# When an attention loop lets in its other work: pieces kept out of the steps in which VectorE masks both pairs

## The chip, the cores and the metric

The kernel runs on one core of one Trainium2 chip. The metric is the device time of one execution in microseconds (us): before the change the median of three runs is 4116.18 us (4115.72 to 4121.67). TensorE (PE) multiplies, VectorE (DVE), ScalarE (ACT) and GpSimd (POOL) work on what comes out, and SyncE (SP) issues transfers. GpSimd has no part in reading the accumulators: in this kernel it only works on tiles that ScalarE or VectorE has written.

## The reference

Three graph-attention layers and one closing layer work on 16 graphs of 1024 nodes with 128 features; one adjacency matrix serves all.

```python
# layers 0, 1, 2: eight heads of 16 features
Q = (h @ Wq).reshape(B, N, 8, 16); K = ...; V = ...
scores = jnp.einsum('bnhd,bmhd->bhnm', Q, K) / jnp.sqrt(16.)
attn = jax.nn.softmax(jnp.where(mask, -jnp.inf, scores), axis=-1)
x = _layer_norm(h + (einsum('bhnm,bmhd->bnhd', attn, V) @ Wo + bo), ln1_g, ln1_b)
x = _layer_norm(x + (jax.nn.relu(x @ W1 + b1) @ W2 + b2), ln2_g, ln2_b)
# layer 3: one head; the score is s_i + s_j through a leaky ReLU
h = x @ W;  e = leaky((h @ a_src)[:, :, None] + (h @ a_dst)[:, None, :])
out = layernorm(softmax(masked e) @ h + x)
```

## The kernel before

**Blocks and steps.** A block is one graph in one of the layers 0 to 2; there are 48, in groups of four graphs (`LANES`): layer 0 of four graphs, then layer 1 of the same four, then layer 2, then the next four graphs. A block has 32 steps: two groups of four heads (`g`) by two halves of the queries (`qh`) by eight tiles of 128 keys (`kt`), so that the step's number modulo 8 is its `kt`. The loop in lines 755 to 795 walks through all 1536 steps. In each it calls, in this order, `score_step`, `av_due` and `piece`.

**A step.** `score_step` (L411) makes two pairs of heads, each a 128x1024 tile of scores in one of three accumulator slots (`s`). A pair is masked in one of two ways. On GpSimd: ScalarE takes the exponential from the slot (L426), and GpSimd multiplies it with a 0/1 mask (L427). On VectorE: VectorE adds a large negative mask while it reads the slot (L429), and ScalarE takes the exponential later (L441). The second pair is always masked on VectorE. The first goes to GpSimd, but for three of the eight key tiles:

```python
BOTH_ON_DVE = (2, 5, 7)
on_pool = pp == 0 and kt not in BOTH_ON_DVE
```

So VectorE has two masks in steps with `kt` 2, 5 and 7 and one in the other five. `av_due` multiplies with the values, four steps later (`AHEAD`), into one accumulator (`acc`, a single buffer). After the last `kt` of a half, `finish` (L449) has VectorE transpose the sums out of it.

**The other work** is cut into pieces. A block's projections (`proj_tasks`, L353) are eight pieces for the next block: two transposes (`t0`), two halves each of K and Q (`split`, where ScalarE writes a rounded part `hi` and VectorE the rest `lo`), two halves of V. What follows a block's attention (`post_tasks`, L465) is eleven: `both` (transposes of the sums on VectorE), two halves of the output projection (`out_proj`: VectorE adds and takes statistics, GpSimd normalises), two transposes (`x1t`), four halves of the first feed-forward product (`ffn1`) and two of the second (`ffn2`). The closing layer (`last_tasks`, L537) is twelve for each graph. All pieces use the one accumulator bank `t` (L134): a piece on TensorE can't start before the last one has been read out of it.

**When a piece runs.** `put` appends pieces to a chain, with a gap in steps that each keeps to the one before. `piece` (L682) is called at the end of each step and takes the first piece, over the chains in order, whose gap has passed; at most one is taken. `need` (L687) takes pieces at once until a mark is reached. `proj_tasks` of the next block enter at the head in step 6. Line 780 asks for them to be done in step 19 (24 in the first block), and `stack` (L397) is emitted there: 16 transfers within the chip which lay `hi` and `lo` out for the first four heads of the next block.

The orders on TensorE and ScalarE are those of the program (`manual_schedule`). Those on VectorE, GpSimd and SyncE are made by a scheduler, with a head start for what frees the bank `t` (`soon`).

In most blocks that lie away from the closing layers, the rule gives this pattern ("." is no piece; `op` is `out_proj`, `f1` is `ffn1`; kt 2, 5 and 7 in brackets):

```
kt           0      1      (2)    3      4      (5)    6      (7)
step  0-7    .      .      .      .      .      both   op0    t0(0)
step  8-15   t0(1)  Wk0    op1    Wk1    .      Wq0    .      Wq1
step 16-23   x1t0   V0     V1     x1t1   f1     f1     f1     f1
step 24-31   ffn2   ffn2   .      .      .      .      .      .
```

Of the kernel before, what the change touches and what calls it, by code (L numbers as in the profile page):

```python
# [28 lines left out]
SOON = 120  # L29
LANES = 4  # L30
FIRST = 1
AHEAD = 4
BOTH_ON_DVE = (2, 5, 7)
TILES = {"w": 10, "x": LANES + 1, "last": 2}
# [77 lines left out]
def fast_path(ctx: ExitStack, tc: tile.TileContext, a: dict, out: bass.AP, flag):  # L112
# [3 lines left out]
    NT = N // P  # L116
# [40 lines left out]
    def fetch(b):  # L157
        def run():
            state["x", b] = load_x(b)
        return run  # L160
# [60 lines left out]
    def first_weights():  # L221
        W[0].update(load_layer(nc, nc.sync, const, a, 0, ("Wo", "b2", "W1", "b1", "W2", "ln1_g", "ln2_g")))
        norm_weights(nc.sync, 0)
# [5 lines left out]
    def other_weights():  # L229
        for l in range(1, L):  # L230
            W.append(load_layer(nc, nc.sync, const, a, l, [n for n in LAYER if n not in ("ln1_b", "ln2_b")]))
            norm_weights(nc.sync, l)
        nc.sync.dma_start(ln2_b_last, rows_of(a[f"L{L - 1}_gnn_ln2_b"]))
        for n in LAST:
            src = a[f"L3_gnn_{n}"]
            if n == "W":
                t = w_nodes[:, :D]
                nc.sync.dma_start(t, src)
            elif n in ("a_src", "a_dst"):
                t = const.tile([P, 1], F32, name=n)  # L240
                nc.sync.dma_start(t, src.rearrange("(p o) -> p o", o=1))
            else:
                t = const.tile([P, D], F32, name=n)
                nc.sync.dma_start(t, rows_of(src))
            wl[n] = t

    def biases():
        for l in range(L):
            if l:
                add_bias(nc.sync, "ln2_b", l - 1, "bo", l)  # L250
            add_bias(nc.sync, "ln1_b", l, "b2", l)

    def last_weights():
        a2 = const.tile([P, 2], F32)
        nc.vector.tensor_copy(a2[:, 0:1], wl["a_src"])
        nc.vector.tensor_copy(a2[:, 1:2], wl["a_dst"])
        ps = bank()
        nc.tensor.transpose(ps[:, :P], w_nodes[:, :D], identf)
        w3t = work.tile([P, P], F32, tag="row", name="w3t", bufs=2)
        nc.vector.tensor_copy(w3t, ps[:, :P])  # L260
        ps = bank()
        nc.tensor.matmul(ps[:, :2], w3t, a2, start=True, stop=True)
        nc.vector.tensor_copy(w_nodes[:, D:], ps[:, :2])
# [133 lines left out]
    def stack(m, g):  # L397

        for pp in range(2):
            for n, order in (("Wk", (0, 1, 0, 1)), ("Wq", (0, 0, 1, 1))):  # L400
                t = work.tile([P, N], F32R, tag=n, name=n, bufs=4)
                r0 = (g * J + 2 * pp) * HD
                for i, part in enumerate(order):
                    behind["stack"] = nc.sync.dma_start(t[i:P:4, :].bitcast(F32), state[n, m][part][r0:r0 + 2 * HD, :].bitcast(F32)).ins
                state[n, g, pp] = t
# [5 lines left out]
    def score_step(step):  # L411
        m, g, qh, kt = step
        e = e_tile()
        q0 = qh * 512
        for pp in range(2):
            q, k = state["Wq", g, pp], state["Wk", g, pp]
            ps = slot()
            for r in range(2):
                nc.tensor.matmul(ps[:, r * 512:(r + 1) * 512], k[64 * r:64 * r + 64, kt * P:(kt + 1) * P],  # L419
                                 q[64 * r:64 * r + 64, q0:q0 + 512], start=True, stop=True)  # L420
            ev = e[:, 2 * pp:2 * pp + 2, :]
            psv = ps.rearrange("p (r q) -> p r q", q=512)
            on_pool = pp == 0 and kt not in BOTH_ON_DVE
            m = (mask01 if on_pool else mask_add)[:, kt, q0:q0 + 512][:, None, :].to_broadcast([P, 2, 512])
            if on_pool:
                nc.scalar.activation(ev, psv, AF.Exp, scale=HD ** -0.5)  # L426
                behind["pool"] = nc.gpsimd.tensor_mul(ev, ev, m).ins  # L427
            else:
                behind["dve"] = nc.vector.tensor_add(ev, psv, m).ins  # L429
                masked.append((2 * step_no[0] + pp + (kt not in BOTH_ON_DVE), ev))  # L430
        step_no[0] += 1
        exponentials()
        return e
# [217 lines left out]
    blocks = [(b, l) for p in range(0, B, LANES) for l in range(L) for b in range(p, p + LANES)]  # L651
    chains = []
    done = {("fetch", b) for b in range(2)}
    now = [0]
# [3 lines left out]
    def put(tasks, mark, chain=None, first=False):  # L658

        if chain is None:  # L660
            chain = {"due": now[0], "queue": deque()}
            chains.insert(0 if first else len(chains), chain)
        for n, task in enumerate(tasks):
            chain["queue"].append(task + (mark if n == len(tasks) - 1 else None,))
        return chain

    def take(chain):

        gap, f, tiles, mark = chain["queue"][0]
        if any(free[t[1:]] == 0 for t in tiles.split() if t[0] == "+"):  # L670
            return False
        chain["queue"].popleft()
        f()
        for t in tiles.split():
            free[t[1:]] += -1 if t[0] == "+" else 1
        done.add(mark)
        chain["due"] = now[0]
        if not chain["queue"]:
            chains.remove(chain)
        return True  # L680

    def piece():  # L682
        for chain in chains:
            if now[0] >= chain["due"] + chain["queue"][0][0] and take(chain):
                return

    def need(mark):  # L687
        while mark not in done:
            first = next(c for c in chains if any(q[3] == mark for q in c["queue"]))
            assert take(first) or any(take(c) for c in list(chains) if c is not first)  # L690
# [63 lines left out]
    with tc.manual_schedule(engines={mybir.EngineType.PE, mybir.EngineType.Activation}):  # L754
        for m, (b, l) in enumerate(blocks):
            order = [(g, qh) for g in range(G) for qh in range(2)]
            if m in (0, len(blocks) - 1):
                order.sort(key=lambda x: x[1])
            for at, (g, qh, kt) in enumerate((g, qh, kt) for g, qh in order for kt in range(NT)):
                now[0] = n  # L760
                if at == (6 if m == 0 else 1):
                    stack(m, 1)
                if n == 6:
                    with tc.issue_after(behind["stack"]):
                        first_weights()
                        other_weights()
                if n == 20:
                    with tc.issue_after(behind["pool"]):
                        biases()
                if n == 40:  # L770
                    with tc.issue_after(behind["dve"]):
                        last_weights()
                if at == 0 and m + 2 < len(blocks) and blocks[m + 2][1] == 0:
                    put([(0, fetch(blocks[m + 2][0]), "+x")], ("fetch", blocks[m + 2][0]))
                if m + 1 < len(blocks):
                    if at == 6:
                        need(("post",) + (blocks[m + 1][0], blocks[m + 1][1] - 1) if blocks[m + 1][1] else
                             ("fetch", blocks[m + 1][0]))
                        put(proj_tasks(m + 1), ("proj", m + 1), first=True)
                    if at == (24 if m == 0 else 19):  # L780
                        need(("proj", m + 1))
                        stack(m + 1, 0)
                step = m, g, qh, kt
                if FIRST <= n < FIRST + 4:

                    with tc.manual_schedule(engines={mybir.EngineType.DVE}):
                        e = score_step(step)
                        neighbours(4 + n - FIRST)
                        masks(4 + n - FIRST, mask_rows(4 + n - FIRST))
                else:  # L790
                    e = score_step(step)
                waiting.append((step, e, n + AHEAD))
                av_due(n)
                piece()
                n += 1
        exponentials(0)
        for n in range(n, n + 2 * AHEAD):
            now[0] = n
            av_due(n)
            piece()  # L800
        while chains:
            now[0] += 1
            for chain in list(chains):
                if now[0] >= chain["due"] + chain["queue"][0][0]:
                    take(chain)
# [236 lines left out]
```

## Time and profile before

| | |
|---|---|
| span of the profiled run | 4114.1 us |
| TensorE busy | 3809.8 us (93%) |
| VectorE, ScalarE, GpSimd busy | 3405.7 (83%), 3393.8 (82%), 3445.6 (84%) |
| score step's masks on VectorE (L429) | 2112 of 1211 ns |
| masks on GpSimd (L427) | 960 of 2149 ns |
| exponentials (L441, L426) | 2112 of 1062 ns, 960 of 1023 ns |

Busy time is the time in which at least one instruction of the engine is under way. Matmuls overlap each other, so their mean durations don't add up, and their ends are modelled; the gaps on TensorE and the time from one step to the next say more than its busy share. The rows of an instruction group give its count, its busy time, the mean of one, and the idle time of its engine just before it with what ended that.

### The profile page before, as it was taken

To read this page: it belongs to the slowest core of one execution; us is meant where nothing else is said; L and a number is where in the kernel's file an instruction comes from. 1 tells how busy PE (TensorE), PEld (TensorE's weight loads), DVE (VectorE), ACT (ScalarE), POOL (GpSimd) and SP (SyncE) were. 2 spreads that over 40 slices of the span, in tenths; PEclk is the share of its full clock that TensorE was granted. 3 is DMA by queue.
4 is the path that set the end of the run, shared out by engine and by line. 5 is a ranking of instruction groups with operands and counts; after the bars stand their busy time and mean duration, and the time that the engine had idled before them with its cause. 6 is when DMAs were issued, how large, how long until landed. Compare 5 with 4: busy or idle time off the path is not lost.

```text
span 4114.1 us, 107861 instructions
## 1 busy us (share of the span) xinstructions
PE 3809.8 (93%) x44501; PEld 1545.5 (38%) x44501; DVE 3405.7 (83%) x5326; ACT 3393.8 (82%) x3961; POOL 3445.6 (84%) x3010
## 2 busy tenths in 40 slices
PE   7999999999999999999999999999999999999996
PEld 2333333344443333334444333333434433333445
DVE  6888888888887888888888888888888888888874
ACT  7999999977778999997777899998777789999760
POOL 5888888888888888887888888888888888888884
PEclk8999999999999999999999999999999999999997
DMA  6221222222211221221222221221222112222100
GB/s 158 61 63 48 57 63 54 51 53 59 64 51 50 63 63 48 57 63 48 59 54 55 61 60 45 63 63 43 53 74 54 48 47 58 62 54 51 51 20 19
DMA packets 124465, 233.13 MB, mean 57 GB/s; under 512 B 34624, under 2 KB 73792, under 8 KB 123968
## 3 DMA queue, kind: packets, MB, share of 16 engines
q1 hardware_dynamic: 122960, 225.71, 21.9%
q8 instruction: 354, 5.80, 0.6%
q14 instruction: 143, 1.17, 0.1%
q10 hardware_dynamic: 1008, 0.44, 0.0%
HBM read 15.54 MB, written 8.39 MB: 6 GB/s over the span
## 4 chain that ended last, share of the span: by engine, by line
PE 49%; DVE 19%; ACT 12%; POOL 11%; issue 9%; ACTq 0%; DMA 0%; SPq 0%; DVEq 0%; POOLq 0%
PE t L293 19%; PE acc L446 15%; PE s L419 12%; DVE e L429 11%; POOL e L427 6%; ACT e L426 5%; ACT e L441 5%; DVE st L318 2%; PE t L282 2%; DVE lo L382 1%; POOL x L337 1%; DVE x L325 1%; ACT xT L287 1%; DVE tt L457 1%; POOL x L341 1%
## 5 line engine op out<-in xcount | busy, mean ns | idle before, releaser
L429 DVE TENSOR_TENSOR e<-s,mask_add 128x1024 f32<-128x1024 f32 x2112 | 2499.5, 1211 | 406.7 <-PE s L419 321.1
L441 ACT ACTIVATE e<-e 128x1024 f32<-128x1024 f32 x2112 | 2196.5, 1062 | 365.0 <-DVE e L429 340.0
L427 POOL TENSOR_TENSOR e<-e,mask 128x1024 f32<-128x1024 f32 x960 | 2048.6, 2149 | 391.3 <-ACT e L426 376.8
L446 PE MATMUL acc<-e,v 128*17 128x512 f32 x12288 | 1628.5, 602 | 63.4 <-DVE tt L457 32.6
L419 PE MATMUL s<-Wq,Wk 64*128 64x512 f32 x6144 | 1206.6, 458 | 83.4 <-ACT e L426 34.6
L426 ACT ACTIVATE e<-s 128x1024 f32<-128x1024 f32 x960 | 982.3, 1023 | 190.9 <-PE s L419 174.7
L419 PEld LDWEIGHTS s<-Wq,Wk 64*128 64x128 f32 x6144 | 499.3, 185 | 1068.9 <-DVE e L429 430.6
L446 PEld LDWEIGHTS acc<-e,v 128*17 128x17 f32 x12288 | 208.0, 95 | 578.6 <-issue 463.6
L337 POOL TENSOR_SCALAR x<-x,mv 128x128 f32<-128x128 f32 x896 | 389.2, 448 | 24.0
L341 POOL TENSOR_TENSOR x<-x,ln_g 128x1024 f32<-128x1024 f32 x97 | 229.3, 2364 | 33.3 <-PE t L282 33.3
L293 PE MATMUL t<-hd,e 128*32 128x129 f32 x8192 | 243.3, 276 | 4.7 <-DVE x L621 3.2
L335 POOL TENSOR_TENSOR mv<-mv,half_neg 128x4 f32<-128x4 f32 x224 | 231.9, 1035 | 18.5
L293 PEld LDWEIGHTS t<-hd,e 128*32 128x32 f32 x8192 | 226.1, 110 | 23.1 <-DVE x L325 4.9
L325 DVE TENSOR_TENSOR x<-t,x 128x512 f32<-128x512 f32 x192 | 131.7, 686 | 91.6 <-PE t L293 90.7
L293 PE MATMUL t<-x1T,W 128*32 128x512 f32 x1536 | 203.9, 603 | 3.0 <-ACT x1T L287 1.5
L318 DVE BATCH_NORM_STATS2 st<-x 128x6 f32<-128x128 f32 x896 | 196.7, 279 | 3.0
L282 PE MATMUL t<-identf,x 128*128 128x128 f32 x888 | 147.2, 289 | 55.2 <-DVE lo L382 27.2
L293 PEld LDWEIGHTS t<-W,hT 128*32 128x32 f32 x6144 | 172.5, 111 | 63.6 <-issue 26.3
L333 POOL TENSOR_SCALAR mv<-mv 128x4 f32<-128x4 f32 x224 | 52.8, 236 | 164.0 <-DVE mv L320 136.3
L293 PE MATMUL t<-W,hT 128*32 128x128 f32 x6144 | 187.1, 274 | 2.7 <-DVE x L325 1.9
L282 PEld LDWEIGHTS t<-identf,x 128*128 128x128 f32 x888 | 94.6, 142 | 250.0 <-issue 93.7
L606 DVE SCALAR_TENSOR_TENSOR e<-s,mask 128x1024 f32<-128x1024 f32 x128 | 150.5, 1209 | 4.8 <-PE s L603 4.1
(97 smaller groups left out, 2488.2 us busy)
## 6 DMA issues: line engine op xcount, KB each, us to landing
Wk<-hi SPq DMA_DIRECT2D x384, 128.0 KB
Wk<-lo SPq DMA_DIRECT2D x384, 128.0 KB
Wq<-hi SPq DMA_DIRECT2D x384, 128.0 KB
Wq<-lo SPq DMA_DIRECT2D x384, 128.0 KB
x<-in_x_dram SPq DMA_DIRECT2D x16, 512.0 KB
out_dram<-x SPq DMA_DIRECT2D x31, 256.0 KB
ai<-in_adj_dram SPq DMA_DIRECT2D x8, 512.0 KB
g_rows<-parts SPq DMA_DIRECT2D x120, 4.0 KB
```

Of the source, the lines that this page charges most:

```text
L282: nc.tensor.transpose(ps[:, t * P:(t + 1) * P], src[:, 4 * h + t, :], identf)
L293: nc.tensor.matmul(dst[j:j + SLOT, :], lhsT[:, j:j + SLOT], rhs, start=start, stop=stop)
L318: nc.vector.bn_stats(st[:, t, :], z[:, t, :])
L335: nc.gpsimd.tensor_tensor(v, v, half_neg[:, ts], OP.pow)
L337: nc.gpsimd.tensor_scalar(z[:, t, :], z[:, t, :], mv[:, t, 0:1], mv[:, t, 1:2], op0=OP.add, op1=OP.mult)
L341: nc.gpsimd.tensor_mul(z, z, rows(gain, n))
L419: nc.tensor.matmul(ps[:, r * 512:(r + 1) * 512], k[64 * r:64 * r + 64, kt * P:(kt + 1) * P], q[64 * r:64 * r + 64, q0:q0 + 512], start=Tru ...
L426: nc.scalar.activation(ev, psv, AF.Exp, scale=HD ** -0.5)
L427: behind["pool"] = nc.gpsimd.tensor_mul(ev, ev, m).ins
L429: behind["dve"] = nc.vector.tensor_add(ev, psv, m).ins
L441: nc.scalar.activation(ev, ev, AF.Exp, scale=HD ** -0.5)
L446: nc.tensor.matmul(acc[j * SLOT:j * SLOT + HD + 1, :], v_bufs[m % 2][:, kt, 2 * j + g, :], e[:, j, :], start=first, stop=last)
```

## The change

It keeps pieces out of the steps with kt 2, 5 and 7 as long as fewer than 20 pieces wait in all chains, and only ahead of the last four blocks (step 1408). The projections then take longer to get through, so the point at which they must be done, and at which `stack` is emitted for the next block, moves from step 19 to step 24 of a block.

```diff
 FIRST = 1
+FEW = 20
 AHEAD = 4
...
     def piece():
+        few = sum(len(c["queue"]) for c in chains) < FEW and now[0] < (len(blocks) - LANES) * 4 * NT
+        if few and now[0] % NT in BOTH_ON_DVE:
+            return
         for chain in chains:
             if now[0] >= chain["due"] + chain["queue"][0][0] and take(chain):
                 return
...
-                    if at == (24 if m == 0 else 19):
+                    if at == 24:
                         need(("proj", m + 1))
                         stack(m + 1, 0)
```

## The prediction

> **What bounds the kernel now.** I read the busy shares first, then the stretches of one common block, then the order of time around its gaps.
>
> ```profile
> PE 3809.8 (93%) x44501; PEld 1545.5 (38%) x44501; DVE 3405.7 (83%) x5326; ACT 3393.8 (82%) x3961; POOL 3445.6 (84%) x3010
> ```
>
> Four engines above 80% and none at the end of its room: what counts is how their loads meet in time. The next view has busy times by stretch: first the four quarters (8 steps each) of one common block, then that block, then the 12 steps around the seam to the next block (steps 26 to 5), then its steps 17 to 23.
>
> ```profile
> core 0: us, PE busy (x) PEld busy (x) DVE busy (x) ACT busy (x) POOL busy (x), PEclk, DMA share, GB/s
> 561.21:577.22 16.01, 15.46 (x136) 5.18 (x132) 15.26 (x18) 15.50 (x17) 14.00 (x9) 1.00 0.53 129
> 577.22:598.24 21.02, 19.01 (x165) 5.89 (x164) 18.94 (x35) 18.61 (x22) 18.69 (x20) 1.00 0.04 8
> 598.24:618.84 20.60, 19.64 (x205) 7.13 (x201) 14.93 (x15) 20.05 (x25) 18.12 (x11) 1.00 0.39 97
> 618.84:637.32 18.48, 17.54 (x228) 7.42 (x225) 16.22 (x32) 15.31 (x17) 16.15 (x19) 1.00 0.03 5
> 561.21:637.32 76.11, 71.65 (x724) 25.63 (x721) 65.36 (x97) 69.46 (x79) 66.97 (x57) 1.00 0.23 57
> 625.62:648.58 22.96, 21.46 (x150) 5.90 (x146) 22.33 (x31) 21.53 (x23) 21.38 (x23) 1.00 0.37 92
> 601.55:618.84 17.29, 17.29 (x186) 6.28 (x185) 12.35 (x12) 16.93 (x21) 14.81 (x9) 1.00 0.34 84
> ```
>
> The bound changes within a block. In the last row a piece runs in every step and TensorE has no gap (17.29 of 17.29), while VectorE idles 5 us. In the row before, 11 of 12 steps have no piece for TensorE (step 5 has only VectorE's `both`): VectorE is busy 22.33 of 22.96, and a step takes 1.91 us. The second quarter is the worst: 21.02 us, and TensorE has gaps although pieces wait. The order of time on TensorE shows why (steps 8 to 11; in brackets idle time and its releaser):
>
> ```profile
> 579.58 0.66 PE L282 MATMUL t<-identf,x 128*128 128x128 f32 x4 [0.33 <-ACT xT L287]
> ...
> 582.11 1.07 PE L293 MATMUL t<-xT,Wk 128*32 128x512 f32 x8
> 583.10 0.73 PE L419 MATMUL s<-Wq,Wk 64*128 64x512 f32 x4
> 583.77 1.05 PE L446 MATMUL acc<-e,v 128*17 128x512 f32 x8
> 585.69 1.08 PE L293 MATMUL t<-Wo,aT 128*32 128x128 f32 x32 [0.87 <-DVE lo L382]
> ```
>
> `op1` sits in a step with kt 2. It needs the bank, which the K projection of the step before holds until VectorE has written `lo`; VectorE's timeline says when:
>
> ```profile
> 583.72 1.23 DVE L429 TENSOR_TENSOR e<-s,mask_add 128x1024 f32<-128x1024 f32 x1 [1.38 <-PE s L419]
> 584.86 0.68 DVE L382 TENSOR_TENSOR lo<-t,hi 128x512 fp32r<-128x512 f32 x1
> 585.46 1.22 DVE L429 TENSOR_TENSOR e<-s,mask_add 128x1024 f32<-128x1024 f32 x1
> ```
>
> `lo` stands between the two masks of that step, and all TensorE's later work waits behind `op1`.
>
> **TensorE's floor.** A step without a piece and without a gap takes 1.645 us (561.21 to 562.85). The same reading of gapless steps gives what a piece adds: 0.86 for K, Q and `ffn1` (2.505), 0.87 for V and `out_proj`, 0.59 for transposes, 1.745 for `ffn2`. It closes on the last row above: 7 x 1.645 + 2 x 0.87 + 0.59 + 4 x 0.86 = 17.29. A common block: 32 x 1.645 + 4 x 0.59 + 8 x 0.86 + 4 x 0.87 + 2 x 1.745 = 68.85 us against 76.11 measured. So 7.26 us are lost. By steps: 3.2 in steps 26 to 4, the stretch without pieces; 4.0 in steps 8, 9, 10, 12 and 16 (0.71, 0.43, 1.08, 0.72, 1.07), which follow or hold a piece in a crowded step, or wait for GpSimd.
>
> **What the Trainium skill says.** "Perfetto Trace Analysis", section "Identifying the Most-Contended Engine": matmul busy time is a poor measure of the room left, since matmuls are pipelined. This trace agrees: 71.65 busy, but 68.85 is enough. Its section "Optimization Strategy" advises interleaving regimes in which different engines are the most contended: this is what the two last rows above show (VectorE 97% in one, 71% in the other). Its section "Matmuls" asks for independent groups to rotate through banks, so that one is read out while the next is computed; here one bank serves all pieces, and the 0.87 us above is the price.
>
> **The change part by part.** Writing out the piece rule for both kernels over all 1536 steps gives 426 of 1072 pieces in steps with kt 2, 5 or 7 before, and 205 of 1072 after. For a common block (2 to 8) the new pattern is:
>
> ```
> kt           0         1      (2)  3      4    (5)  6      (7)
> step  0-7    f1        ffn2   .    ffn2   .    .    both   .
> step  8-15   t0(0)     t0(1)  .    Wk0    op0  .    Wk1    .
> step 16-23   Wq0       op1    .    Wq1    .    .    V0     .
> step 24-31   V1,x1t0   x1t1   .    f1     f1   .    f1     .
> ```
>
> Nothing is added or removed; only places move. Loads by quarter, with VectorE's mask at 1.13 (three in 3.48 us), `lo` 0.60, a half of `out_proj` or `ffn2` 1.68, `finish` 0.8, `both` 1.4; ScalarE's exponential 0.94 (three in 2.95), transposes 0.67, `hi` and V 0.47, `ffn1` 0.58:
>
> - before: TensorE 14.6, 18.1, 19.5, 16.7; the largest of the three engines by quarter 16.3, 18.1, 19.5, 16.7: 70.6.
> - after: TensorE 17.5, 16.9, 16.6, 17.8; the largest 17.9 (VectorE), 17.3 (ScalarE), 16.6, 18.5 (ScalarE): 70.3.
>
> So by quarters nothing is won: TensorE gets level, but `ffn2` and `both` crowd VectorE in the first, and transposes and `ffn1` ScalarE in the last. What can be won is what is lost inside the quarters, 76.1 - 70.6 = 5.5 us. New losses, step by step:
>
> - `op0` right after the first half of K (kt 3 and 4): the same meeting as `op1` above, as VectorE's new order again has a mask ahead of `lo`: 1.1.
> - second transpose after the first: 0.7, as in step 8 now.
> - `op1` after the first half of Q: here `lo` is ahead of the mask: 0.4. `x1t0` after V1 in one step: ScalarE alone reads V out, a score and a value product lie between: 0.3.
> - steps without a piece: 14 instead of 13, but single ones between steps in which TensorE is behind, and VectorE (1.13 + 0.60 against 2.5 us of TensorE) catches up: I take a third of 3.2, 1.0. Between 0 (fully hidden) and 3.2 (nothing).
> - accumulator handed over after kt 3, and GpSimd's late masks: 0.5. A piece now nearly always follows kt 3's products, and its 0.86 lies beside VectorE's 0.70 transpose.
>
> Sum 4.0, so 72.9 us for such a block, 3.2 less. After the first closing layers the pattern is shifted (a backlog of about seven pieces stays, one transpose sits in kt 7, `both` is forced in step 11); I take 4.6, so 2.6 less. Eight blocks of the first kind and 17 of the second (15 to 20, 27 to 32, 39 to 43): 8 x 3.2 + 17 x 2.6 = 70 us.
>
> Blocks with closing layers:
>
> ```profile
> 1157.20:1256.60 99.40, 93.31 (x1361) 44.13 (x1360) 81.00 (x136) 74.45 (x85) 82.73 (x77) 1.00 0.23 58
> ```
>
> There 20 or more pieces wait, so the old rule holds; backlog moves a block later, at the same sum: 0. The last four blocks and the end keep their rule: 0.
>
> The move of `stack`: 0. Before, its transfers were issued from 596.29 to 607.8, as their inputs came, and were read first at 637.32. Now the last Q half is written some 4 steps later, about 9 us; 20 us of room remain. Queued behind it on SyncE are the other half's transfers, which start after the block's end, and the closing layers' small rows, which have eight steps.
>
> 4116.2 - 70 = 4046 us.
>
> **Rivals.**
> - Nearly all fine losses go (2 us left): 25 x 5.3 = 132, 3984 us. For it: VectorE has 5 us idle in the dense stretch. Against: ScalarE is at 69.46 of 76.11 and would have to run at 98% of 70.9.
> - VectorE and ScalarE take over by quarters (17.9 and 18.5 above come on top of losses as now): 0.8 a block, 25 x 0.8 = 20: 4096 us. For it: the quarter sums, 70.6 and 70.3. Against: six tiles of `e` and four steps of delay let an engine lag some 4 us.
> - Slower: 41 steps hold two or more pieces instead of 11, nine of the forced ones are projections in step 24, and pieces in neighbouring steps meet at the one bank. At 1 us more in 25 blocks: 4141 us. Against: the waits of steps 10, 12 and 16 lose their cause.
>
> **How the numbers follow.** 0.5 for 4046, 0.16 for the nearly full gain, 0.17 for the small one, 0.15 slower, 0.02 for no movement at all. The small gain lies at 0.5% and may end within 0.2% (0.03 of it): faster 0.80, same 0.05, slower 0.15. The range goes from the nearly full gain, 3985, to the upper side of the small one, 4110.
>
> **What would show it.** Right: common blocks at 72 to 74 us and all alike; TensorE's waits on `lo` (L382) down; VectorE's busy share per block spread over the quarters; blocks with closing layers and the end as before. Wrong: common blocks at 76 or more, with TensorE waiting for VectorE's or ScalarE's scores in the first and last quarter; long waits at step 0 for `Wk` or `Wq` transfers; or closing blocks that grow by what the common ones gain.

## The result and the profile after

The changed kernel takes 4097.74 us, median of four runs (4097.01 to 4099.05); the kernel before, run beside it, 4118.15 (4115.72 to 4121.67). The ratio is 0.995, with a 95% interval from 0.9933 to 0.9967: 20 us less, where the prediction had 70 less. The direction was right, the size was not, and the time is that of the rival "small gain" (4096).

The page of the kernel after, its busy shares (line numbers of the kernel after are one higher than before for everything behind the new constant):

```profile
PE 3818.2 (93%) x44501; PEld 1548.0 (38%) x44501; DVE 3393.5 (83%) x5326; ACT 3381.9 (83%) x3961; POOL 3450.5 (84%) x3010
```

Nothing moves here; all four engines do what they did. The stretches of one common block (block 6: its four quarters, then the whole) answer to the rows shown of before:

```profile
core 0: us, PE busy (x) PEld busy (x) DVE busy (x) ACT busy (x) POOL busy (x), PEclk, DMA share, GB/s
475.98:495.51 19.53, 18.52 (x236) 7.55 (x233) 17.54 (x36) 16.55 (x18) 15.08 (x17) 1.00 0.44 109
495.51:514.56 19.05, 17.65 (x156) 5.90 (x152) 16.23 (x24) 17.33 (x21) 18.81 (x15) 1.00 0.00 1
514.56:534.02 19.46, 18.71 (x212) 6.92 (x208) 17.99 (x27) 18.12 (x21) 18.43 (x19) 1.00 0.43 110
534.02:551.29 17.27, 17.23 (x132) 5.18 (x128) 12.97 (x13) 17.27 (x22) 14.79 (x8) 1.00 0.00 1
475.98:551.29 75.31, 72.11 (x724) 25.55 (x720) 64.72 (x97) 69.28 (x79) 67.11 (x57) 1.00 0.23 57
```

Before, the quarters took 16.01, 21.02, 20.60 and 18.48 us; now 19.53, 19.05, 19.46 and 17.27. The work is level, and yet the block takes 75.31 instead of 76.11. The last quarter comes within 0.35 us of its floor (8 x 1.645 + 2 x 0.59 + 3 x 0.86 = 16.92); the other three lose 2.0 to 2.1 us each.

The balance over all 1536 steps uses the prediction's own measure, each step's time less TensorE's floor for it (1.645 us, and the pieces' prices), so that pieces which only moved from one block to another don't count:

| blocks | lost before | lost after | change | forecast |
|---|---|---|---|---|
| 1 to 8 | 60.0 | 54.1 | -5.9 | -26 |
| 15 to 20, 27 to 32, 39 to 43 | 135.2 | 109.3 | -25.8 | -44 |
| 9 to 14, 21 to 26, 33 to 38 (closing layers) | 152.4 | 157.9 | +5.4 | 0 |
| 44 to 47 | 38.6 | 41.4 | +2.9 | 0 |

The absolute losses of the last two rows hang on the prices taken for the closing layer's pieces, which the prediction doesn't give; the changes hardly do.

Block 0 and the start gain another 1.1, and the stretch behind the last step is 5.4 longer with the same work in it (114.25 us at a granted clock of 0.79 before, 119.66 at 0.77 after). Part of these 5.4 may be no effect of the change: `at24_only` below, which runs the same pieces in the same steps as the kernel before, takes 116.3 there. Together, each figure rounded by itself, that is the 19.0 us by which the two profiled spans differ. So the common blocks brought 31.7 of the 70 us, and 12.6 went back elsewhere.

**Where block 6 still loses its 6.45 us.** Step by step, time less floor: steps 5 to 8 lose 2.19, step 12 (`op0` after `Wk0`) 1.33, step 17 (`op1` after `Wq0`) 0.50, steps 21 and 22 1.0; 1.4 more is spread over the rest, at most 0.3 in a step. Steps 8 and 22 hold a piece again; the lag of the empty steps ahead of them still shows there. What happens in steps 4 to 8 is seen in VectorE's order of time:

```profile
start us, us, engine line op out<-in xcount [idle before <-releaser]
486.83 1.19 DVE L430 TENSOR_TENSOR e<-s,mask_add 128x1024 f32<-128x1024 f32 x1
487.94 0.68 DVE L326 TENSOR_TENSOR x<-t,x 128x512 f32<-128x512 f32 x1
488.54 0.24 DVE L460 RECIPROCAL recs<-tt 128x16 f32<-128x16 f32 x1
488.69 0.83 DVE L319 BATCH_NORM_STATS2 st<-x 128x6 f32<-128x128 f32 x4
489.44 0.36 DVE L321 BATCH_NORM_AGGREGATE mv<-st 128x2 f32<-128x6 f32 x4
489.72 4.58 DVE L430 TENSOR_TENSOR e<-s,mask_add 128x1024 f32<-128x1024 f32 x4
494.22 0.70 DVE L474 STREAM_TRANSPOSE aT<-A 128x512 f32<-128x512 f32 x1
494.84 0.30 DVE L350 TENSOR_REDUCE chk<-recs 128x1 int32<-128x64 int32 x2
495.07 3.47 DVE L430 TENSOR_TENSOR e<-s,mask_add 128x1024 f32<-128x1024 f32 x3
```

No line has an idle time: the second half of `ffn2` (add, statistics), seven masks and `both` follow each other without a gap. TensorE, which has no piece in steps 4 to 7, waits for the masks:

```profile
490.96 0.50 PE L420 MATMUL s<-Wq,Wk 64*128 64x512 f32 x2 [0.26 <-DVE e L430]
492.09 0.50 PE L420 MATMUL s<-Wq,Wk 64*128 64x512 f32 x2 [0.63 <-DVE e L430]
...
496.33 0.51 PE L420 MATMUL s<-Wq,Wk 64*128 64x512 f32 x2 [0.32 <-DVE e L430]
```

The blocks of the second kind show the same at another place. In block 18 both halves of `out_proj` come in steps 22 and 24 and nothing follows until step 30; the stretch of steps 24 to 28:

```profile
1533.64:1545.16 11.52, 9.86 (x97) 3.40 (x94) 11.52 (x27) 9.99 (x12) 10.34 (x15) 1.00 0.00 0
```

VectorE is busy for the whole 11.52 us. TensorE's floor there is 5 x 1.645 + 0.87 = 9.10, so 2.4 of that block's 5.6 us are lost here.

### The profile page after: what moved, and what is told of

Its sections match the earlier page's. It is cut to its first block, busy times and chain, and to the rows that moved or that the text cites. A ratio compares the mean times of both kernels' runs of the same rounds, so it can differ in the third digit from the quotient of the medians.

```text
span 4095.1 us, 107716 instructions
## 1 busy us (share of the span) xinstructions
PE 3818.2 (93%) x44501; PEld 1548.0 (38%) x44501; DVE 3393.5 (83%) x5326; ACT 3381.9 (83%) x3961; POOL 3450.5 (84%) x3010
## 4 chain that ended last, share of the span: by engine, by line
PE 43%; DVE 21%; POOL 14%; ACT 14%; issue 6%; SPq 0%; DMA 0%; ACTq 0%; DVEq 0%; POOLq 0%
PE t L294 17%; PE acc L447 14%; DVE e L430 12%; PE s L420 11%; ACT e L442 7%; POOL e L428 7%; ACT e L427 4%; POOL x L338 3%; DVE st L319 2%; POOL mv L336 2%; DVE lo L383 2%; PE t L283 1%; DVE tt L458 1%; ACT hT L503 1%; POOL x L342 1%
## 5 line engine op out<-in xcount | busy, mean ns | idle before, releaser
L294 PE MATMUL t<-hd,e 128*32 128x129 f32 x8192 | 253.7, 282 | 21.7 <-DVE lo L383 15.8
L342 POOL TENSOR_TENSOR x<-x,ln_g 128x1024 f32<-128x1024 f32 x97 | 230.0, 2371 | 32.0 <-PE t L283 31.7
L294 PEld LDWEIGHTS t<-hd,e 128*32 128x32 f32 x8192 | 234.9, 113 | 42.1 <-DVE lo L383 21.7
L336 POOL TENSOR_TENSOR mv<-mv,half_neg 128x4 f32<-128x4 f32 x224 | 232.6, 1038 | 18.5
L383 DVE TENSOR_TENSOR lo<-t,hi 128x512 fp32r<-128x512 f32 x188 | 128.0, 681 | 32.9 <-ACT hi L382 32.5
```

What stands on the lines that cost most here:

```text
L294: nc.tensor.matmul(dst[j:j + SLOT, :], lhsT[:, j:j + SLOT], rhs, start=start, stop=stop)
L336: nc.gpsimd.tensor_tensor(v, v, half_neg[:, ts], OP.pow)
L342: nc.gpsimd.tensor_mul(z, z, rows(gain, n))
```

## The experiments

**What belongs to the change: the move of `stack` alone, and the rule without it.** `at24_only` is the old rule with `stack` in step 24; `few_at19` the new rule with the projections still asked for in step 19.

```diff
# at24_only, against the kernel before
-                    if at == (24 if m == 0 else 19):
+                    if at == 24:
# few_at19, against the kernel after
-                    if at == 24:
+                    if at == (24 if m == 0 else 19):
```

> The old rule for pieces, with the stacking of the next block emitted in step 24 in all blocks. The pieces stand where they stood before; only the layout transfers' place in their queue moves. Theory A (the transfers have some 20 us of room): 4118, within 0.2% of before. Rival B (the place of the transfers sets the start of a block): the first step of common blocks grows, 4130 or more, or shrinks, 4105 or less.

> The new rule for pieces, but the projections are asked for in step 19 as before. In a common block the last half of Q and both halves of V are then forced in one go at step 19, three pieces through one bank with nothing between them. Theory A (what a piece waits for is the bank, read out by VectorE and ScalarE): each of the two handovers costs TensorE about 1 us, so common blocks take 76.5 to 77.5 us and the kernel 4120 to 4150. Rival B (only the number of pieces per stretch counts): common blocks stay near 75 and the kernel near 4098.

`at24_only`: 4121.1 us, ratio 1.0009 [1.0, 1.0018]; its blocks are those of before (76.1). The move alone costs nothing and brings nothing. `few_at19`: 4269.57 us, 1.0371 [1.0354, 1.0389]; common blocks 81.4 to 82.5, far above the 76.5 to 77.5 expected. Its step 18 takes 8.8 us, 4.55 over its floor, since three pieces that the rule held back are forced there at once and meet at the one bank:

```profile
556.65 1.04 PE L294 MATMUL t<-xT,Wq 128*32 128x512 f32 x8
559.90 1.47 PE L294 MATMUL t<-Wv,xT 128*32 128x128 f32 x32 [2.20 <-DVE lo L383]
562.05 1.94 PE L294 MATMUL t<-Wv,xT 128*32 128x128 f32 x32 [0.68 <-ACT v L389]
```

What the expectation lacked is step 8 of the same block, which loses another 2.7 us: VectorE stands idle for 1.98 us ahead of the transpose of `both`, for GpSimd's `A`, a wait that comes up again in `spread` below. So the later `stack` is no gain of its own but what the rule needs.

**Which steps, and which pieces.** `bar036` closes three other steps, evenly spaced too; `dve_pieces` closes kt 2, 5 and 7 only to pieces with work for VectorE; `few100` lifts the limit of 20.

```diff
# bar036
-        if few and now[0] % NT in BOTH_ON_DVE:
+        if few and now[0] % NT in (0, 3, 6):
# dve_pieces
+ON_DVE = ("split", "both", "out_proj", "ffn2", "nodes", "edges", "two", "aggregate")
...
+        crowded = few and now[0] % NT in BOTH_ON_DVE
...
+            if crowded and any(w in chain["queue"][0][1].__qualname__ for w in ON_DVE):
+                continue
# few100
-FEW = 20
+FEW = 100
```

> The new rule and step 24, but pieces are kept out of the steps with kt 0, 3 and 6, where GpSimd masks one pair, and let into 2, 5 and 7. As many steps are closed and the pieces are as far apart. Theory A (what matters is that VectorE has two masks in kt 2, 5 and 7): common blocks lose 8 us or more and take 77 or more, the kernel 4120 to 4160. Rival B (what matters is that pieces are spread evenly): common blocks at 74.5 to 75.5, the kernel at 4090 to 4105.

> The new rule, but only pieces with work on VectorE (projections of K and Q, out_proj, ffn2, both, and most of the closing layer) are kept out of kt 2, 5 and 7; transposes, V and ffn1, which ScalarE alone reads out, may run there. The steps without pieces gather again in steps 0 to 5. Theory A (VectorE's own pieces meeting its two masks are what costs): common blocks at 74 to 75.5, the kernel at 4080 to 4100. Rival B (what the change wins, it wins by even spacing): common blocks back at 76, the kernel at 4110 to 4120.

> The changed kernel with 100 for 20 in the rule: no piece ever runs in kt 2, 5 and 7 before the last four blocks, blocks with closing layers included. Theory A (closing pieces crowd VectorE and the bank just as much there, and every step closed to them only defers work that TensorE has to do anyway): blocks with closing layers lose no more than now, the loss of their large pieces moves to later blocks, kernel 4080 to 4110. Rival B (backlog has a price: forced pieces and a heap at the end): 4120 or more.

`bar036`: 4311.47 us, 1.0465 [1.0447, 1.0482], blocks at 79 to 84: pieces spread out evenly don't do it, which steps stay free matters. Its loss is larger than expected, and whether VectorE's two masks alone make it is not shown: the largest single wait in its block 6, 2.0 us in step 4, is for VectorE's transpose of the accumulator, which also comes at a fixed key tile. `dve_pieces`: 4107.48, 0.9972 [0.996, 0.9983]; most common blocks of both kinds are at 75.4, almost the 75.3 of the kernel after, but without what its second kind of block wins (74.5). The blocks are as expected, the kernel isn't (4080 to 4100). `few100`: 4296.25, 1.0437 [1.0421, 1.0453]: common blocks stay at 75.3 and the closing blocks heap up (109.8 and 126.8 us in blocks 13 and 14, where the kernel after has 101.4 and 95.8). The limit is needed.

**Is VectorE's crowd in steps 5 to 8 the loss?** Three attempts. `spread` pulls the `ffn2` halves apart; `pool5` gives one mask of step 5 to GpSimd in blocks 1 to 8; `bare5` leaves that mask out altogether, in blocks 5 to 8 that of step 21 as well, so it doesn't do the whole work. In `pool5` and `bare5` ScalarE then reads the slot in VectorE's place.

```diff
# spread
-        together = [..., (5, x1t(0), "+w"), (1, x1t(1), "+w")]
-        together += [(1, ffn2(0), "-w -w"), (1, ffn2(1), "-w -w")]
+        together = [..., (3, x1t(0), "+w"), (1, x1t(1), "+w")]
+        together += [(1, ffn2(0), "-w -w"), (4, ffn2(1), "-w -w")]
# pool5
-            on_pool = pp == 0 and kt not in BOTH_ON_DVE
+            on_pool = pp == 0 and (kt not in BOTH_ON_DVE or (0 < step[0] < 9 and (g, qh, kt) == (0, 0, 5)))
# bare5
+UNMASKED = {m: (5,) if m < 5 else (5, 21) for m in range(1, 9)}
...
+            bare = pp == 0 and step_at[0] in UNMASKED.get(step[0], ())
+            if bare:
+                nc.scalar.activation(ev, psv, AF.Exp, scale=HD ** -0.5)
```

> The changed kernel with two gaps altered: the second half of ffn2 four steps after the first (one before), the first transpose of x1 three steps after out_proj (five before). In common blocks 2 to 8 the two halves of ffn2 then stand in steps 0 and 4 instead of 1 and 3, both in 6. The work is the same. Theory A (what is left in these blocks is VectorE falling behind where its own pieces stand close: 2.2 us in steps 5 to 8 and 1.0 in 21 and 22 of 6.5 us lost): the loss in steps 5 to 8 falls below 1.2, common blocks 2 to 8 take 73.5 to 74.7, and the kernel 4070 to 4092. Rival B (each quarter's sums of VectorE and ScalarE set the time, and they hardly change): common blocks stay at 75.0 to 75.6, the kernel 4092 to 4105.

> The changed kernel, but in blocks 1 to 8 the first pair of step 5 is masked on GpSimd instead of VectorE: 1.13 us less on VectorE where it is behind after ffn2 and both, 2.15 us more on GpSimd, which is busy 15.1 of 19.5 us in that quarter. Theory A (VectorE's queue is what TensorE waits for in steps 5 to 8, 2.2 us): blocks 2 to 8 take 74.0 to 74.6 instead of 75.3, about 1 us less each. Rival B (ScalarE and GpSimd are as near to their limit, the wait moves to them): 75.0 or more.

> The changed kernel, in which one pair isn't masked at all: the first pair of step 5 in blocks 1 to 8, in blocks 5 to 8 that of step 21 as well. ScalarE takes the exponential from the slot; 1.13 us of VectorE's work are gone in that step and nothing is put on GpSimd. Theory (crowding of VectorE loses 2.2 us in steps 5 to 8 and 1.0 in steps 21 and 22): steps 5 to 8 fall from 9.35 to about 8.2 with step 9 staying at 2.3, blocks 2 to 4 at about 74.2; in blocks 5 to 8 steps 21 and 22 fall from 5.15 to 4.2 to 4.4 as well, blocks at about 73.2 to 73.5. Rival (the bound there is something else, ScalarE or the bank): blocks 75 or more, or the time returns within a few steps, as it did with the mask on GpSimd.

`spread` fits neither expectation: 4207.42 us, 1.0222 [1.0208, 1.0236], blocks at 78 to 80. It doesn't tell whether the crowd matters, since the new places made a wait of another kind. VectorE's order of time in its steps 4 to 6, and GpSimd's:

```profile
505.13 0.71 DVE L474 STREAM_TRANSPOSE aT<-A 128x512 f32<-128x512 f32 x1 [3.52 <-POOL A L461]
505.76 0.65 DVE L326 TENSOR_TENSOR x<-t,x 128x512 f32<-128x512 f32 x1
506.34 1.21 DVE L430 TENSOR_TENSOR e<-s,mask_add 128x1024 f32<-128x1024 f32 x1
```

```profile
500.25 4.27 POOL L428 TENSOR_TENSOR e<-e,mask 128x1024 f32<-128x1024 f32 x2
504.47 0.63 POOL L461 TENSOR_TENSOR A<-tt,recs 128x256 f32<-128x256 f32 x1
```

The transpose of `both` stands at the head of VectorE's queue, `ffn2`'s add and the masks stand behind it, and what it waits for stands behind two masks on GpSimd.

`pool5`: 4099.85 us, 0.9962 [0.9947, 0.9977], no gain. Yet steps 5 to 8 fell from 9.35 to 8.22 us, by 1.13, exactly the mask's time. Step 9 grew from 2.26 to 3.69, with TensorE's values waiting 1.39 us for GpSimd (stretches of steps 5 to 8, step 9 and the whole block 6):

```profile
490.97:499.19 8.22, 7.62 (x56) 2.29 (x52) 8.22 (x16) 7.74 (x10) 7.87 (x11) 1.00 0.00 0
499.19:502.88 3.69, 2.30 (x18) 0.85 (x17) 1.43 (x2) 3.48 (x5) 3.69 (x2) 1.00 0.00 0
477.98:553.58 75.60, 71.69 (x725) 25.52 (x722) 63.59 (x96) 69.38 (x79) 69.11 (x58) 1.00 0.23 57
```

`bare5`: 4087.36 us, 0.9923 [0.9908, 0.9938]. The same stretches of its block 3:

```profile
262.65:270.88 8.23, 7.65 (x58) 2.30 (x54) 8.23 (x16) 7.75 (x10) 7.88 (x11) 1.00 0.00 0
270.88:273.14 2.26, 2.26 (x18) 0.85 (x17) 1.42 (x2) 2.26 (x4) 2.26 (x2) 1.00 0.00 0
249.66:323.83 74.17, 71.71 (x724) 25.51 (x720) 63.62 (x96) 69.13 (x79) 67.01 (x57) 1.00 0.24 58
```

Steps 5 to 8 again fall by 1.13, step 9 keeps its 2.26, and the block has 74.17: a microsecond of VectorE's work taken from this stretch is a microsecond of the block. Blocks 2 to 8 together win 9.4 us. Block 1, where steps 5 and 6 lose nothing in the kernel after, wins nothing (74.9 instead of 73.1). VectorE is still busy all of the 8.23 us, so 1.13 of the 2.19 us is shown to be its crowd; the rest is read from the trace alone. At step 21 the theory holds only in part: steps 21 and 22 fell from 5.15 to 4.81 where 4.2 to 4.4 was expected, and the blocks to 73.6 to 74.1.

**What holds `op0` in step 12?** The prediction put its wait down to a VectorE mask ahead of `lo`. The order of time at that place in the kernel after (steps 11 to 12, ScalarE, VectorE and the waiting product):

```profile
504.25 1.04 ACT L427 ACTIVATE e<-s 128x1024 f32<-128x1024 f32 x1
...
505.16 1.07 ACT L442 ACTIVATE e<-e 128x1024 f32<-128x1024 f32 x1
...
505.66 1.23 DVE L430 TENSOR_TENSOR e<-s,mask_add 128x1024 f32<-128x1024 f32 x1
...
506.11 0.60 ACT L382 CAST hi<-t 128x512 fp32r<-128x512 f32 x1
...
506.80 0.68 DVE L383 TENSOR_TENSOR lo<-t,hi 128x512 fp32r<-128x512 f32 x1
...
507.62 1.08 PE L294 MATMUL t<-Wo,aT 128*32 128x128 f32 x32 [1.08 <-DVE lo L383]
```

There are two suspects: the mask at 505.66 on VectorE, and the two exponentials at 504.25 and 505.16 which ScalarE, in the program's order, takes before `hi`. K's products end at about 504.85. `pool12` removes the first suspect (both masks of step 12 on GpSimd in blocks 1 to 8), `exp_after` the second in the whole kernel (exponentials after the piece), and `exp_after_old` makes that edit on the kernel before.

```diff
# pool12
-            on_pool = pp == 0 and kt not in BOTH_ON_DVE
+            on_pool = pp == 0 and kt not in BOTH_ON_DVE or (0 < step[0] < 9 and (g, qh, kt) == (0, 1, 4))
# exp_after, exp_after_old
     def score_step(step):
...
         step_no[0] += 1
-        exponentials()
         return e
...
                 piece()
+                exponentials()
```

> The changed kernel, but in blocks 1 to 8 both pairs of step 12 (kt 4) are masked on GpSimd, so that no mask stands between the K projection's rest (lo) and out_proj's first half on VectorE. Theory A (out_proj waits for the bank because lo stands behind a mask: 1.33 us lost in step 12): step 12 falls from 3.85 us to 2.7 to 3.0, blocks 2 to 8 to 74.2 to 74.8. Rival B (the bank's wait is that of ScalarE's rounding ahead of lo, or GpSimd's added 2.15 us come back as a wait for a masked tile): step 12 stays above 3.5, or the block at 75.0 or more.

> The changed kernel, with each step's exponentials of VectorE-masked pairs emitted after the step's piece instead of ahead of it, so that ScalarE reads the bank t out first (hi, transposes, halves of V, ffn1). Theory (op0 in step 12 and op1 in step 17 wait because hi is queued on ScalarE behind two exponentials of its own step): step 12 falls from 3.85 to about 2.9 us, step 17 from 3.0 to about 2.6, the chain of waits on lo shrinks, common blocks 73.8 to 74.5 instead of 75.3, kernel 4060 to 4080. Rival (the later exponentials give their time back as waits for e or for the values' products): step 12 shrinks but its neighbours grow, common blocks 75 or more, kernel 4095 or more.

> The same edit on the kernel before. If the order on ScalarE ahead of hi was also behind the wait of op1 in step 10 (1.08 us lost), step 10 falls by about 0.5 to 1 and common blocks from 76.1 to about 75, kernel 4070 to 4095. If there the wait was for VectorE's mask ahead of lo, as the prediction read it, step 10 stays and the kernel is within 0.3% of 4118.

`pool12`: 4094.64 us, 0.9949 [0.9934, 0.9964]. VectorE now stands idle and waits for `hi`:

```profile
504.49 0.69 DVE L383 TENSOR_TENSOR lo<-t,hi 128x512 fp32r<-128x512 f32 x1 [1.11 <-ACT hi L382]
...
505.24 1.08 PE L294 MATMUL t<-Wo,aT 128*32 128x128 f32 x32 [0.94 <-DVE lo L383]
```

Step 12 went only from 3.85 to 3.72: the mask was worth 0.13 of the 1.33 us. In `exp_after` step 12 takes 3.01; block 6 again:

```profile
501.52 0.60 ACT L382 CAST hi<-t 128x512 fp32r<-128x512 f32 x1
...
501.99 1.09 ACT L441 ACTIVATE e<-e 128x1024 f32<-128x1024 f32 x1
502.15 0.69 DVE L383 TENSOR_TENSOR lo<-t,hi 128x512 fp32r<-128x512 f32 x1 [0.40 <-ACT hi L382]
...
502.90 1.08 PE L294 MATMUL t<-Wo,aT 128*32 128x128 f32 x32 [0.23 <-DVE lo L383]
```

One exponential now stands behind `hi` instead of ahead of it, and the wait is 0.23 instead of 1.08. Common blocks take 74.1 instead of 75.3, within the 73.8 to 74.5 expected; step 12 gives 0.84 of it, while step 17 falls by 0.49 and step 16 grows by 0.61. The kernel is not as expected: 4110.86 us, 0.9984 [0.9977, 0.9991]. Blocks 9 to 14 take 554.7 instead of 545.4 and blocks 21 to 26 555.1 instead of 547.8. On the kernel before the edit costs: 4170.24, 1.013 [1.0113, 1.0147]. There step 10, where `op1` waits, stayed at 3.59 us to the hundredth. The order of time in block 7, as in the prediction's lines, shows why:

```profile
595.07 0.59 ACT L381 CAST hi<-t 128x512 fp32r<-128x512 f32 x1
595.54 1.23 DVE L429 TENSOR_TENSOR e<-s,mask_add 128x1024 f32<-128x1024 f32 x1 [1.04 <-PE s L419]
...
596.68 0.68 DVE L382 TENSOR_TENSOR lo<-t,hi 128x512 fp32r<-128x512 f32 x1
```

In the kernel before, `hi` began 0.6 us after K's products (583.79 against 583.18). Here it begins right behind them (595.07 against 595.00), and `lo` comes no earlier, as it stands behind the mask. So for that step the prediction's reading (VectorE's mask ahead of `lo`) stands.

**Keeping that gain.** `exp_few` uses the new order only where the change's rule holds, `exp_first` only in blocks 1 to 8 and where it holds.

```diff
# exp_few; exp_first asks in both places for a block from 1 to 8 as well
         step_no[0] += 1
-        exponentials()
+        if not few_wait():
+            exponentials()
...
+    def few_wait():
+        return sum(len(c["queue"]) for c in chains) < FEW and now[0] < (len(blocks) - LANES) * 4 * NT
...
+                late = few_wait()
                 av_due(n)
                 piece()
+                if late:
+                    exponentials()
```

> As exp_after, but the exponentials go after the piece only where the changed rule holds (fewer than 20 pieces waiting, ahead of step 1408); elsewhere the order is the changed kernel's. Theory (the later exponentials shorten the common blocks by taking ScalarE's queue away from hi, and what exp_after lost lies in the blocks with closing layers and the last four): common blocks 74.0 to 74.2, blocks 9 to 14, 21 to 26 and 33 to 38 within 1 us of the changed kernel's, kernel 4078 to 4090, faster than both. Rival (the closing blocks' loss comes from what the common blocks hand on): closing blocks grow as in exp_after, kernel 4100 or more.

> As exp_few, but only in blocks 1 to 8 the exponentials go after the piece; from block 9 on the program is the changed kernel's. Theory (what it wins there, 1.2 us in each of blocks 2 to 8, comes through when nothing after them is touched): blocks 1 to 8 at about 592 us together instead of 600.5, the rest as in the changed kernel, 4086 to 4091, faster than both kernels. Rival (the blocks with closing layers give it back whatever their own order is): 4094 or more, with blocks 9 to 14 above 547 together.

`exp_few`: 4094.05 us, 0.9937 [0.9924, 0.9951], less than expected: blocks 2 to 8 win 1.2 each, but the second kind of block goes from 74.5 to 74.9, and blocks 9 to 14, 21 to 26 and 33 to 38 grow by 0.9 to 1.6 us a group, the first of them within the spread of kernels that are alike there (545.4 to 547.6). `exp_first`: 4089.84 us (4085.24 to 4091.12), 0.9921 [0.9907, 0.9934], the fastest complete kernel of the study. Blocks 1 to 8 take 591.4 us together instead of 600.5; blocks 9 to 43 take 2925.9 instead of 2922.9. Four kernels whose edits don't reach those blocks (`to_end`, `bare5`, `pool12`, `pool5`) take 2923.8 to 2925.4 there, so most of these 3 us is no more than the spread from one kernel to the next.

**GpSimd's product into `A`.** In the kernel after, a new loss outside the common blocks is in step 0 of block 45, where VectorE stands idle 2.2 us ahead of the transpose of `both`, as in `spread`. `asoon` gives that product a head start, `spread_asoon` does so with `spread`'s places.

```diff
-            nc.gpsimd.tensor_mul(state["A"][:, qh, :, g, :], tt[:, :, :HD],
-                                 rec[:, :, None].to_broadcast([P, 16, HD]))
+            with soon():
+                nc.gpsimd.tensor_mul(state["A"][:, qh, :, g, :], tt[:, :, :HD],
+                                     rec[:, :, None].to_broadcast([P, 16, HD]))
```

> The changed kernel, with GpSimd's product into A (finish) given the head start that frees the bank. Theory (VectorE's first transpose of both stands at the head of VectorE's queue while GpSimd still has masks ahead of A, 2.2 us in step 0 of block 45): waits of aT for A fall, blocks 44 and 45 lose 1 to 2 us less, common blocks 75.0 to 75.3, kernel 4085 to 4098. Rival (A only trades places with a mask, whose products then wait): the same within 0.2%, with longer waits of the values' product for GpSimd's masks.

> As asoon, with the second ffn2 half four steps after the first and x1t three after out_proj, so that ffn2, ffn2 and both don't follow each other within five steps. In spread alone VectorE stood 3.5 us ahead of aT for GpSimd's A (4207 us). If that wait is what spoilt it and crowding of VectorE in steps 5 to 8 is what limits the changed kernel: steps 4 to 8 lose below 1.2 us in all, common blocks 73.5 to 74.7, kernel below 4085. If the crowd is not the limit, or A still comes late: 75 or more, and the trace shows which of the two, by VectorE's idle time ahead of aT.

`asoon`: 4098.36 us, 0.9954 [0.9937, 0.9971], every block as in the kernel after within 0.3 us but for two at +1.5 and +0.8, and VectorE's idle time ahead of `aT` for `A` unchanged (14.0 us in 7 waits). `spread_asoon`: 4210.7, 1.0226 [1.0209, 1.0243], and VectorE is still idle for 3.5 us in steps 4 to 6 of its block 4. The head start doesn't bring `A` forward far enough; whether `spread`'s places would help with `A` in time stays open.

**The last four blocks.** Blocks 44 and 45 take 10.9 us more than before. `to_end` keeps the new rule there.

```diff
-        few = sum(len(c["queue"]) for c in chains) < FEW and now[0] < (len(blocks) - LANES) * 4 * NT
+        few = sum(len(c["queue"]) for c in chains) < FEW
```

> The changed kernel, with the new rule in the last four blocks too. Blocks 44 and 45 lost 10.8 us to the kernel before. Theory (7.5 of it is backlog that the new rule has put off and that must be worked off somewhere): blocks 44 and 45 become common ones (about 75 and 81) and the time reappears in blocks 46 and 47 or behind the last step; kernel 4097 to 4115. Rival (the change back to the old rule costs it): the last four blocks together get 5 us or more shorter, kernel 4085 to 4093.

4098.75 us, 0.9948 [0.9933, 0.9964]. Stretches: blocks 44 and 45, then all the rest, first in the kernel after, then in `to_end`.

```profile
3625.05:3788.97 163.92, 152.96 (x1616) 56.63 (x1613) 134.98 (x212) 143.57 (x163) 146.03 (x130) 0.98 0.22 53
3788.97:4095.14 306.17, 254.45 (x4063) 138.23 (x4062) 203.75 (x409) 152.24 (x208) 215.32 (x224) 0.89 0.11 30
```

```profile
3626.44:3782.10 155.66, 150.03 (x1610) 55.44 (x1606) 132.40 (x203) 141.82 (x162) 142.74 (x123) 1.00 0.22 56
3782.10:4097.72 315.62, 255.92 (x4074) 140.61 (x4070) 206.64 (x418) 153.38 (x208) 218.16 (x231) 0.90 0.12 29
```

8.3 us leave the first stretch and 9.5 appear in the second. The end of the rule costs nothing; it is where pieces that were put off are worked off. The 3 us lost there beyond that floor, and the 5.4 behind the last step, aren't settled: the stretch behind the last step has the same instructions in four kernels with this end (the kernel after, `asoon`, `pool12`, `exp_first`) and takes from 116.6 to 121.1 us in them, at granted clocks from 0.77 to 0.80.

## Why the prediction was right or wrong

- **Floor and pattern: right.** The pieces fell where the rule was written out, TensorE's floor of 68.85 us held (the last quarter comes near its share), and levelling the quarters went with only 0.8 us in block 6, where its sums of 70.6 and 70.3 had next to nothing. One of these sums was too dear: the last quarter ran in 17.27 us, where ScalarE alone was to take 18.5. "Perfetto Trace Analysis" of the Trainium skill, section "Optimization Strategy", says that interleaving regimes may improve performance; here it levelled the quarters to within 2.3 us and gave 0.5%.
- **The move of `stack`, 0: right** (`at24_only`, 1.0009).
- **The step that failed: "steps without a piece ... I take a third of 3.2, 1.0".** It held that the empty steps would be single and that VectorE would catch up in them. In block 6 they, with steps 8 and 22 behind them, lose 3.2 us (2.19 in steps 5 to 8, 1.0 in 21 and 22), which was the upper bound given there. That is 2.2 of the 2.45 us missed in such a block. The pattern printed in the prediction shows why: steps 4 to 7 hold nothing for TensorE, but VectorE has `ffn2`'s second half, `both` and six masks in that time. VectorE doesn't catch up in such a step, it is what the step waits for. `bare5` shows it for steps 5 to 8 (1.13 us of VectorE taken, 1.13 us of time gone), less cleanly for step 21, and the trace alone speaks for it in steps 24 to 28 of the second kind of block, which lose 2.4 us. That it is VectorE's time, and not its turn at the slot that ScalarE takes over in `bare5`, is not tested apart; that `pool5` and `bare5` give back just the mask's time speaks for it.
- **`op0` after `Wk0`, 1.1: size near by luck, cause wrong.** It lost 1.33. Mainly not the mask ahead of `lo` but ScalarE's exponential ahead of `hi` held it: `pool12` against `exp_after`, 0.13 against 0.84 us. The wait in step 10 before had the other cause, as `exp_after_old` shows; the two places look alike in the order of pieces.
- **`op1` after `Wq0`, 0.4: right** (0.50). **The transposes, 0.7 and 0.3: too dear**; steps 9 and 24 lose nothing.
- **The sum for a block.** Forecast loss 4.0, measured 6.45 for the first kind; 4.6 against 5.6 for most blocks of the second. Over eight and seventeen blocks that is 38 of the 51 us missed. Its working had a gap of its own: the 4.0 was laid on TensorE's floor of 68.85, although its quarter sums had just put the fullest engines at 70.3, and the 1.45 us between the two had no term.
- **Closing blocks, the last four and the end, 0: too good.** They lose 5.4, 2.9 and 5.4 us more. That backlog moves a block later at the same sum was right for the pieces themselves (`to_end`), not for the waits that they meet; which waits these are no run isolates, and the last 5.4 may in part be no effect of the change.
- **Signs named ahead.** Common blocks at 72 to 74 us: no, 75.3 and 74.5. Waits on `lo` down: for the products, yes. The idle time that ended on `lo`, before and after (total, times, longest); PE rows are of the products, PEld rows of the weight loads, which overlap products:

```profile
PE t L293 <- DVE lo L382: 35.6, 40, 1.4
PE t L282 <- DVE lo L382: 27.2, 33, 1.5
PEld t L293 <- DVE lo L382: 31.7, 61, 1.5
```

```profile
PE t L294 <- DVE lo L383: 45.1, 58, 2.4
PE t L283 <- DVE lo L383: 4.8, 4, 1.4
PEld t L294 <- DVE lo L383: 95.8, 127, 2.6
```

The products' idle time fell from 62.8 to 49.9 us, while that of the weight loads rose.

- **One reading was off.** Of the twelve steps 26 to 5, all twelve, not eleven, have no piece for TensorE; no sum rests on it.
- **The rival that came true** has the right number, 4096, and the right engine for the first quarter. In the last quarter, where it had ScalarE, 0.35 us is lost. That the number fits so closely is luck in part: the common blocks gained 31.7 us, and 12.6 went back where the rival had nothing. What was held against it, that six tiles of `e` and four steps of delay let an engine lag some 4 us, doesn't help where scores wait for a slot which VectorE has not yet read.

## What to carry to other kernels

A step that holds nothing for the fullest engine is not free: before pieces are moved out of a crowded step, sum up the other engines' work over the few steps around it, not over a quarter of the block, since a stretch of four steps in which VectorE had no gap cost 2.2 us here while its quarter still had room. When a wait names the last instruction of a read-out, follow both of its inputs up their own engines' queues; the instruction that stands ahead of the first read-out on the other engine can be the cause, and it takes one run for each suspect to tell. A local gain (1.2 us a block) should be tried where it was seen and nowhere else first: applied to the whole kernel it came out at 13 us slower than the change alone, in eight blocks at 8 us faster.

## What the runs showed that had not been expected

- A mask given to an engine with room by its share (GpSimd at 67.11 of 75.31 us in the block) moved the wait by one step: 1.13 us won in steps 5 to 8, 1.43 lost in step 9.
- One instruction at the head of VectorE's queue, waiting for GpSimd's product, held masks behind it for 3.52 us (`spread`); altering two gaps by two and three steps was enough to make that wait.
- The same edit, the exponentials behind the piece, made common blocks 1.2 us shorter after the change and 1.3 us longer before it (76.1 to 77.4).
